# Seven block products for eight in three places of a four-layer graph network

## The chip, the cores and the metric

One core of a Trainium2 chip runs the whole program. The metric is device time in microseconds (us), the median of several executions of the same kernel; lower is better. All runs told here were in the fast state. "Rounds" are timed runs of a kernel in turn with the kernel before on the same chip. A ratio is the mean time of one kernel's fast runs over that of the other's in the same rounds, so it is not quite the ratio of the medians quoted beside it.

## The reference, cut to what matters

32 batches pass through four layers of a graph network in float32. A batch has 512 nodes with 128 features and a 512 x 512 adjacency matrix. In outline, with the parts that the change touches:

```python
# layer 2: four projections; the k-th sees the newest features and stored ones
src = nodes @ ws + bs            # 3rd: nodes = [f2, f1], 4th: [f3, f1, f0]
dst = nodes @ wd + bd
src_agg = einsum(src, l2norm(adj, 2)); dst_agg = einsum(dst, l2norm(adj, 1))
f_new = tanh(concat(src_agg, self_rep, dst_agg) @ wu + bu)

# layer 3: a GRU; r and z gates add two products
r = sigmoid(h @ W_hr + m @ W_ir + b_r)
z = sigmoid(h @ W_hz + m @ W_iz + b_z)
```

The rest is cut. h1 is the normed input of layer 1, f0 that of layer 2, f1 to f4 the outputs of layer 2's projections, h and m the state and the message of layer 3. The four weight matrices of such a place form a 2 x 2 block matrix, and the two halves of the 512 nodes make the left side 2 x 2 blocks as well: eight block products.

## The kernel before

The order of instructions is not written down by hand. A planner inside the kernel runs when the program is built: it goes through time with a price for every operation, gives each engine the most urgent ready one, and hands out buffers. The result is one fixed list per engine, and **each engine works through its list strictly in order**. The prices and the rule for buffers matter below:

```python
class Plan:
    RATE, TRANSFER = 240.0, 1.3     # a transfer lands after kb / 240 + 1.3 us
    ...
    # in order(): may this operation take its buffers now?
    older = item[1].batch - min(unfinished)
    if any(len(free[x.kind]) < len([y for y in new if y.kind == x.kind])
           + older * self.kept.get(x.kind, 0) for x in new):
        held.append(item)           # no: looked at again later
        continue

plan = Plan(sb, psum, {"bank": 8, "s2": 32, "s4": 6, "s8": 10},   # places
                      {"bank": 1, "s2": 7, "s4": 0, "s8": 0})     # kept, per older batch
def t_mm(n):  return n * 0.001675 + 0.004
def t_act(n, pointers=0):  return 0.09 + 0.093 * pointers + n / 1150
```

A batch that is not the oldest unfinished one may take a buffer only if `older * kept` of that kind stay free. The large kind, s8, holds the adjacency matrices and the gates.

Two pieces of a batch matter below. `turned` transposes a 512 x 128 matrix: VectorE turns 32 x 32 blocks, four transfers write them to HBM, one reads them back, and ScalarE copies the result into the order that matmuls need. The copy `rows` spreads the norms of the adjacency matrix:

```python
for k in range(NC):
    op("SP", 0.4, lambda k=k: away(k), [blk], [(bounce, {k})], kb=64)
op("SP", 0.4, lambda: nc.sync.dma_start(mT.ap(), bounce.tile), [bounce], [mT], kb=256)
...
op("ACT", t_act(N), lambda: nc.scalar.copy(hT..., turned_cols(t)), [t], [hT])
...
op("ACT", t_act(2 * N), lambda: nc.scalar.copy(
    rows.ap().rearrange("p s (c n) -> p (s c) n", c=NC),
    spaced.ap().rearrange("p n k -> p k n")), [spaced], [rows])
```

The first three and the last two batches transpose on TensorE instead (`at_ends`). A projection of layer 2 (`paired_rows`) makes, for each half of the nodes, products of 256 columns that add up in one PSUM bank, and one VectorE addition of the bias writes `sd`, which the aggregation then uses.

## Time and profile before

| | before |
|---|---|
| median of 4 runs (range) | 2353.82 us (2352.41 to 2356.74) |
| profiled span, granted clock | 2352.6 us, full in the middle |
| TensorE (PE) / VectorE (DVE) / ScalarE (ACT) busy | 2321.2 / 1123.3 / 923.2 us |
| distance of equal batches in the middle | 71.66 us |

The prediction below shows the lines for these. Three more lines also belong here. They are from the list of transfers (`--dma`); the last columns are size and the median us from issue to landing. f4r is the same round trip for f4.

```profile
turned<-turn_turned SPq DMA_DIRECT2D x81, 256.0 KB, 2.6
spaced<-bounce SPq DMA_DIRECT2D x32, 512.0 KB, 4.1
f4r<-turn_f4r SPq DMA_DIRECT2D x27, 256.0 KB, 4.6
```

The planner prices 256 KB at 256 / 240 + 1.3 = 2.37 and 512 KB at 512 / 240 + 1.3 = 3.43 us. So the trace showed before any change that the prices are too low, most of all for f4r.

### The profile page before, as it was taken

How to read it: one execution, taken by the hardware profiler on the slowest of the kernel's cores; microseconds unless marked ns; L12 is line 12 of the kernel's file. 1: busy time of each engine (PE TensorE's matmuls, PEld its weight loads, DVE VectorE, ACT ScalarE, POOL GpSimd, SP SyncE). 2: the span in 40 equal slices, each digit the busy share in tenths (PEclk: the TensorE clock that was granted, in tenths of full speed). 3: DMA queues.
4: the chain of work that ended last, by engine and by line, in shares of the span. 5: the costliest groups of instructions: out<-in, count | busy, mean ns of one | idle time of the engine just before them, and what ended most of it. 6: DMA issues, size and time to landing. Idle time of an engine off the chain costs nothing.

```text
span 2352.6 us, 24187 instructions
## 1 busy us (share of the span) xinstructions
PE 2321.2 (99%) x8466; PEld 1426.5 (61%) x8466; DVE 1123.3 (48%) x2917; ACT 923.2 (39%) x2018; POOL 282.0 (12%) x218
## 2 busy tenths in 40 slices
PE   6999999999999999999999999999999999999998
PEld 4665566566666565665666665656665666656655
DVE  4344444555445555445554445554455544454523
ACT  7424233443334443334443344433344333344312
POOL 3100011111011110011110111110111101111001
PEclk9999999999999999999999999999999999999999
DMA  6112212322313332223223133322233321332000
GB/s 239 59 54 72 72 52 92 108 86 88 99 56 104 90 99 90 75 78 108 90 90 99 50 103 91 98 90 82 72 107 90 98 91 55 98 107 72 17 10 9
DMA packets 127128, 196.36 MB, mean 83 GB/s; under 512 B 18336, under 2 KB 75040, under 8 KB 127008
## 3 DMA queue, kind: packets, MB, share of 16 engines
q1 hardware_dynamic: 126720, 194.71, 27.0%
q8 instruction: 66, 1.08, 0.2%
q14 instruction: 54, 0.44, 0.1%
q10 hardware_dynamic: 288, 0.13, 0.0%
HBM read 157.95 MB, written 36.83 MB: 83 GB/s over the span
## 4 chain that ended last, share of the span: by engine, by line
PE 94%; DVE 2%; ACT 2%; DMA 1%; issue 0%; POOL 0%; SPq 0%; DVEq 0%; POOLq 0%; ACTq 0%
PE ps_agg L289 62%; PE ps_sd L289 18%; PE ps_gate L289 7%; PE ps_upd L289 3%; PE ps_msg L289 1%; PE ps_lin L289 1%; PE ps_node L289 1%; ACT h L417 1%; POOL sc L405 0%; DMA a<-in_adj 0%; ACT sq L581 0%; DVE bn L389 0%; SPq L435 0%; DVE g L659 0%; DMA spaced<-bounce 0%
## 5 line engine op out<-in xcount | busy, mean ns | idle before, releaser
L289 PE MATMUL ps_agg<-aT,sd 128*128 128x512 f32 x1024 | 521.2, 593 | 0.0
L289 PE MATMUL ps_agg<-a,sd 128*128 128x512 f32 x1024 | 501.1, 592 | 0.0
L289 PE MATMUL ps_sd<-w_sb,f 128*128 128x256 f32 x1792 | 484.2, 381 | 1.0 <-ACT f L455 0.8
L490 DVE TENSOR_TENSOR sd<-ps_sd,rf_sb 128x512 f32<-128x512 f32 x256 | 175.9, 687 | 606.7 <-PE ps_sd L289 606.7
L289 PEld LDWEIGHTS ps_sd<-w_sb,f 128*128 128x128 f32 x1792 | 327.1, 191 | 172.8 <-issue 134.0
L405 POOL TENSOR_TENSOR sc<-v,neg_half 128x4 f32<-128x4 f32 (+1 forms) x128 | 180.1, 1408 | 2020.1 <-DVE v L392 1384.0
L417 ACT ACTIVATE h<-xr,nb,sc 128x128 f32<-128x128 f32 x384 | 157.9, 482 | 556.8 <-DVE nb L413 556.6
L289 PEld LDWEIGHTS ps_agg<-a,sd 128*128 128x128 f32 x1024 | 185.4, 191 | 164.3 <-issue 155.3
L289 PEld LDWEIGHTS ps_agg<-aT,sd 128*128 128x128 f32 x1024 | 187.1, 191 | 84.4 <-issue 56.9
L289 PE MATMUL ps_agg<-f,w_sb 128*128 128x512 f32 x448 | 229.7, 594 | 0.0
L619 ACT ACTIVATE f<-ps_agg,cf_sb 128x512 f32<-128x512 f32 x128 | 87.2, 681 | 132.0 <-PE ps_agg L289 131.9
L289 PE MATMUL ps_agg<-aT,rep 128*128 128x512 f32 x256 | 131.4, 595 | 3.6 <-DVE rep L557 3.6
L289 PEld LDWEIGHTS ps_gate<-w_sb,mT 128*128 128x128 f32 x512 | 95.3, 190 | 61.6 <-issue 55.0
L426 DVE STREAM_TRANSPOSE blk<-h 128x512 f32<-128x512 f32 x81 | 57.6, 711 | 154.8 <-ACT h L417 154.8
L289 PE MATMUL ps_agg<-a,rep 128*128 128x512 f32 x256 | 130.7, 592 | 0.0
L289 PE MATMUL ps_agg<-aT,msg 128*128 128x512 f32 x256 | 125.9, 592 | 0.0
L289 PE MATMUL ps_gate<-w_sb,mT 128*128 128x256 f32 (+1 forms) x512 | 123.1, 326 | 0.0
L289 PEld LDWEIGHTS ps_gate<-w_sb,hT 128*128 128x128 f32 x512 | 91.0, 190 | 49.8 <-issue 43.5
L289 PE MATMUL ps_gate<-w_sb,hT 128*128 128x128 f32 (+1 forms) x512 | 119.0, 327 | 0.0
L289 PE MATMUL ps_agg<-aT,h 128*128 128x256 f32 (+2 forms) x384 | 108.8, 380 | 0.0
L603 DVE TENSOR_TENSOR aT<-aT,rows 128x512 f32<-128x512 f32 x128 | 87.8, 687 | 35.4 <-PE ps_agg L289 33.8
L669 ACT ACTIVATE g<-g 128x512 f32<-128x512 f32 (+1 forms) x68 | 41.1, 605 | 156.1 <-DVE g L659 156.1
(101 smaller groups left out, 2724.6 us busy)
## 6 DMA issues: line engine op xcount, KB each, us to landing
aT<-in_adjt SPq DMA_DIRECT2D x124, 512.0 KB, 4.8
a<-in_adj SPq DMA_DIRECT2D x62, 512.0 KB, 4.6
turn_turned<-blk SPq DMA_DIRECT2D x324, 64.0 KB, 1.8
turned<-turn_turned SPq DMA_DIRECT2D x81, 256.0 KB, 2.6
spaced<-bounce SPq DMA_DIRECT2D x32, 512.0 KB, 4.1
x<-in_x SPq DMA_DIRECT2D x32, 256.0 KB, 2.9
out<-xo SPq DMA_DIRECT2D x30, 256.0 KB, 3.0
turn_f4r<-blk SPq DMA_DIRECT2D x108, 64.0 KB, 2.3
```

Source lines behind the costliest of these rows:

```text
L289: op("PE", t_mm(n), lambda: nc.tensor.matmul(out_of(ps.ap()), lhs(), rhs(), start=start, stop=stop), reads, [ps], later=later)
L405: op("POOL", t_pow(n), lambda: nc.gpsimd.tensor_tensor(inv.ap()[:, :n], v8.ap()[:, :n], neg_half[:, :n], op=ALU.pow), [v8, NH], [(inv, {0})])
L417: op("ACT", t_act(D, 2), lambda c=c: nc.scalar.activation(h.ap()[:, c, :], xin.ap()[:, c, :], AF.Relu, bias=nb.ap()[:, c:c + 1], scale=inv ...
L426: op("DVE", t_tt(N), lambda: nc.vector.transpose(blk.ap().rearrange("p b (c r) -> p c b r", c=NC), m.ap().rearrange("p c (b s) -> p c b s" ...
L490: op("DVE", t_tt(N), lambda ps=ps, h=h: nc.vector.tensor_add(sd.ap()[:, 2 * h:2 * h + 2, :], ps.ap().rearrange("p (j v) -> p j v", j=2), a ...
L603: op("DVE", t_tt(N), lambda m=m, c=c, s=s: nc.vector.tensor_mul(m.ap()[:, c, :], m.ap()[:, c, :], rows.ap()[:, s, :]), [(m, {c}), rows], [ ...
L619: op("ACT", t_act(N, 1), lambda ps=ps, i=i, f_new=f_new: nc.scalar.activation(f_new.ap(), ps.ap(), AF.Tanh, bias=cf_sb[:, i:i + 1]), [ps, ...
L669: op("ACT", t_act(cols), lambda s=s: nc.scalar.activation(g.ap()[:, s, :2 * D], g.ap()[:, s, :2 * D], AF.Tanh, scale=0.5), [(g, part)], [( ...
```

## The change

The intent: seven block products (a scheme of Strassen's kind) and some additions on VectorE for eight products on TensorE, which is the bound. Places: layer 2's third projection ("mid"), its fourth ("last"), and the r and z gates of layer 3 ("gates", except in the last two batches). The core of the diff:

```diff
+SEVEN = {"last": 0 * 5 * D, "mid": 1 * 5 * D, "gates": 2 * 5 * D}
-    plan = Plan(..., {"bank": 1, "s2": 7, "s4": 0, "s8": 0})
+    plan = Plan(..., {"bank": 1, "s2": 5, "s4": 0, "s8": 1})
     def t_mm(n):
-        return n * 0.001675 + 0.004
+        return n * 0.00166 + 0.0085
+        def seven(site, x1, x2, dst, part):
+            ... # five buffers s13, s24, ev, dv, xx; four PSUM banks
+            dve(of(s13, 1), lambda: half(x1, 0), lambda: half(x1, 1), [x1], ..., sub=True)
+            product(bank_a, 0, lambda: half(x1, 0), lambda: wt(b11), [x1, wbuf])
+            product(bank_a, 1, of(s13, 1), lambda: t(2), ...)
+            ... # five more products, each two matmuls of 128 columns,
+            ... # and thirteen more VectorE additions
         for i, (wsd, wn) in enumerate(W_L2):
-            sd = paired_rows(f, wsd, W2F, rf_sb, RF, i * 2 * D)
+            if i == 2 and "mid" in SEVEN:
+                sd = buf("s4", (P, NC, 2 * D), "sd")
+                seven("mid", f[1], f[0], *of_halves(sd))
+            elif i == 3 and "last" in SEVEN:
+                sd = paired_rows(f[:1], wsd, W2F, rf_sb, RF, i * 2 * D, early)
+            else:
+                sd = paired_rows(f, wsd, W2F, rf_sb, RF, i * 2 * D)
 ... # (cut) gates alike; combined weights at setup; finer parts of buffers
```

Besides the products, the change alters what the planner keeps back: of the large buffers now one for each older unfinished batch. With 0, the planner finds no end for three places (that version doesn't build). Of the small ones (s2) it keeps 5 instead of 7, and a matmul's price changes a little.

## The prediction

> **What bounds the kernel now.** I read the page first: the engines' shares, then the chain that ended last.
>
> ```profile
> PE 2321.2 (99%) x8466; PEld 1426.5 (61%) x8466; DVE 1123.3 (48%) x2917; ACT 923.2 (39%) x2018; POOL 282.0 (12%) x218
> ...
> PE 94%; DVE 2%; ACT 2%; DMA 1%; issue 0%; POOL 0%; SPq 0%; DVEq 0%; POOLq 0%; ACTq 0%
> ```
>
> TensorE is busy for 2321.2 of 2352.6 us, and 94% of the chain is matmuls. Busy alone doesn't prove a full pipe, since matmuls overlap; so I went on to the chain in order of time and to the busy times of two stretches.
>
> ```profile
> 341.00 8.59 PE ps_agg L289 x20
> 352.16 2.16 PE ps_sd L289 x10
> 370.70 1.34 PE ps_upd L289 x12
> 412.66 8.59 PE ps_agg L289 x20
> ```
>
> ```profile
> 341.00:412.66 71.66, 71.66 (x261) 43.98 (x261) 35.40 (x91) 28.61 (x62) 8.80 (x7) 1.00 0.28 89
> 412.66:484.32 71.66, 71.66 (x261) 43.99 (x261) 35.39 (x91) 28.61 (x62) 8.80 (x7) 1.00 0.30 89
> ```
>
> The same long piece returns every 71.66 us: one batch of the 32. In the second fence the columns are length, then busy (records) of PE, weight loads, VectorE, ScalarE, GpSimd, then clock, DMA share, GB/s. TensorE is busy in all of it and its clock is full. The chain also gives the price of a matmul inside a stream. Each float32 matmul leaves two records. 512 columns: 8.59 / 10 = 0.859 us. 256 columns: 2.16 / 5 = 0.432. 128 columns: 1.34 / 6 = 0.223. For 384 columns the timeline has 0.64.
>
> Does this price list explain a batch? Dividing the record counts of the groups, kept apart by shape, by 64 gives per batch 52 matmuls of 512 columns, 42 of 256, 2 of 384 and 34 of 128: together 130, as the x261 above says. 52 x 0.859 + 42 x 0.432 + 2 x 0.64 + 34 x 0.223 = 71.67 us, against 71.66. So a batch in the middle is the sum of its matmuls and nothing else: what is taken off that sum comes off the time one for one, until something else takes its place. What is not full is the two ends:
>
> ```profile
> PE ps_fold L289 <- DMA raw<-in_raw: 11.1, 1, 11.1
> PE ps_t L453 <- ACT h L417: 3.6, 2, 2.3
> PE ps_agg L289 <- DVE rep L557: 3.6, 3, 1.5
> ```
>
> These are TensorE's largest waits (total, times, longest). All its idle time is 2352.6 - 2321.2 = 31.4 us, of which 11.1 is the first load.
>
> **What the Trainium skill says.** "FP8 and Floating Point Precision", section TensorE Precision Notes: true FP32 takes 4 passes through the array. "TensorE: Matmul & The Clock Gate", section Back-to-back issue gap: an isolated warm gap of N/2.4 + 2.5 ns per instruction. Two records of two passes at 512 columns would be 2 x (2 x 512/2.4 + 2.5) = 858 ns: the trace agrees (859). At 128 columns it would be 218 ns, and the trace has 223; the same section warns that at small N the weight loads are part of the spacing. I take the trace's 223. "VectorE: DVE Perf Modes", section The TRN2 errata: a float32 tensor_tensor add lasts (N + 151)/0.96 ns; 691 ns at 512, which the trace shows (690 for the bias addition after the msg product). For 256 it gives an estimate of 424 ns; the trace has no such shape yet, and between its 340 (128) and 684 (512) a straight line gives 455.
>
> **The change part by part.** In three places a product of a (2x2 blocks) left side with a 2x2 block weight, eight block products, becomes seven plus additions on VectorE.
>
> Removed: per place 8 matmuls of 256 columns, 8 x 0.432 = 3.456 us. Added: 14 of 128 columns (7 products, each for two blocks of 128 rows), 14 x 0.223 = 3.122 us. Saved: 0.334 us a place, less than the eighth of 3.456 (0.432), because 14 short instructions pay the fixed part more often than 8 long ones. The third and fourth projection of layer 2 do it in all 32 batches, the gates in 30 (the last two keep the old form): 94 places. The static order confirms the counts: 752 matmuls of 256 columns go, 1316 of 128 come. 94 x 0.334 = 31.4 us, all on the path by the argument above. In the middle a batch should take 71.66 - 3 x 0.334 = 70.66 us.
>
> VectorE: per place 12 additions of 256 columns and 2 of 512, 12 x 0.424 + 2 x 0.691 = 6.47 us. Gone are 2 of 512 per third projection and 2 per gate site, 124 in all; the fourth projection keeps its two, now adding to the stored half instead of the bias. Sum: 94 x 6.47 - 124 x 0.687 = +523 us, so about 1646 us busy, 71% of the new span; in a middle batch 35.4 + 19.4 - 2.8 = 52 of 70.7 us. That is beside TensorE, not on the path, as long as the answers come in time. ScalarE, GpSimd and the transfers hardly change (one small bias load more). Setup gains 15 additions of 128 columns on VectorE, 15 x 0.34 = 5 us, at a time when it is busy half (24 of the first 50 us).
>
> Does VectorE answer in time? The place that feeds at once is the third projection: its newest input arrives, a subtraction must be ready before the second pair of products, and the sums before the aggregation. Between the first use of that input and the product that needs the subtraction, the order holds 512 + two 128 + 512 columns, 0.859 + 0.446 + 0.859 = 2.16 us, for one addition of 0.42 and a handover. The fourth projection's products start a layer earlier, from inputs known since layer one, so they are filler. A middle batch is the same pattern of matmul rows again and again, and in it a second half of an already begun fourth-projection product (needing only f0 and weights) is left over for 74 rows and run late: the scheduler, which picks the most urgent ready instruction, had ready work throughout. So the order has no planned hole there.
>
> At the ends nothing hides the longer detour through VectorE. The first batches and the last two run with little beside them; I put 1 us for each end, an estimate from the waits above (single waits of 0.5 to 2.3 us there) and from a few more dependent additions of about 0.4 us.
>
> Sum: 2353.8 - 31.4 + 2 = 2324.4; I go to 2323, since some added delay at the ends may fall where TensorE waits anyway.
>
> **The rivals.**
> Weight loads bound the short products. A load lasts 190 ns in the trace and a 128-column record takes only 111 ns of the stream. Were they exposed, a short matmul would cost 2 x 190 = 380 ns and the change would add 1316 x 0.157 = 207 us. Against it: the strings of twelve 128-column matmuls with new stationary blocks each time run at 0.223 us now. I give it almost nothing.
> VectorE becomes the bound, or its answers come late. Its load goes from 49% to some 74% of a batch, in an order fixed beforehand. If each place stalled TensorE by a single late addition (0.33 us), the whole gain would be gone: about 2354. For it: a chain of dependent additions with waits on itself in the order. Against it: the slack above, and that the same scheduler produced a middle without holes before. I expect at most a third of that, 10 us.
> The full arithmetic gain. Without the fixed cost a place saves 0.427 us (256 columns less), 40 us in all: 2314. The trace's 128-column price speaks against it.
> More than 2%: it would need 47 us, more than the arithmetic allows, so 15 us of the 31.4 idle would have to go as well, though 11.1 of them wait for the first load, which is not touched.
>
> **Range and chances.** 2323 us, 1.3% below 2353.8. Downward, better filling at the ends or a price nearer the full gain could bring 7 us: 2316. Upward, stalls in a third of the places and at the ends: 2337. Within 2% means 2306.8 to 2400.9. Faster by over 2%: 0.03; slower: 0.02; within: 0.95.
>
> **What would show it.** Right: equal distance of the chain's long pieces, 70.6 to 70.7 us instead of 71.66, with TensorE busy throughout; the new 128-column products 0.22 us apart; VectorE near 1650 us; TensorE's idle total 31 to 35 us. Wrong: waits of TensorE for VectorE (the s24, s13 or sd pieces) repeating in every batch; a gap between new products above 0.23 us; a beginning or an end that is 5 us or more longer.

## The result, and the profile after

Measured: **2360.76 us** (median of 4, 2356.81 to 2364.68) against 2353.82. The ratio is 1.0028, 95% interval 1.0008 to 1.0048: slower by 0.3%, the same within the 2% limit. The prediction had said 2323 with a range of 2316 to 2337. The time is outside it.

The page of the changed kernel, engines' shares and the chain that ended last:

```profile
PE 2306.8 (98%) x9594; PEld 1440.2 (61%) x9594; DVE 1543.5 (65%) x4124; ACT 937.8 (40%) x2018; POOL 255.6 (11%) x218
...
PE 77%; DMA 9%; DVE 5%; ACT 4%; SPq 2%; issue 1%; POOL 1%; ACTq 0%; POOLq 0%; DVEq 0%
```

TensorE has 14 us less to do by this count, and matmuls fell from 94% to 77% of the chain; transfers, VectorE and ScalarE took the rest. The chain in order of time, and the busy times of one batch and of a long stretch (columns as in the prediction):

```profile
1236.56 6.87 PE ps_agg L295 x16
...
1308.37 6.87 PE ps_agg L295 x16
...
1379.91 6.87 PE ps_agg L295 x16
```

```profile
1236.56:1308.37 71.81, 71.20 (x297) 44.33 (x297) 48.88 (x132) 29.89 (x65) 7.58 (x6) 1.00 0.29 88
600.00:1200.00 600.00, 593.71 (x2473) 369.90 (x2472) 404.28 (x1072) 243.62 (x522) 64.48 (x51) 1.00 0.30 89
```

The equal pieces are 71.81 and 71.54 us apart, not 70.66, and TensorE is no longer full. TensorE's waits, by what it waited for (total, times, longest):

```profile
PE ps_sd L295 <- ACT hT L488: 14.9, 25, 2.0
PE ps_fold L295 <- DMA raw<-in_raw: 10.7, 1, 10.7
PE ps_t L483 <- ACT h L447: 6.0, 5, 2.3
PE ps_sd L295 <- ACT f L488: 4.1, 6, 1.5
PE ps_agg L295 <- POOL diag L618: 2.9, 2, 1.6
PE ps_agg L295 <- DVE sd L522: 2.8, 5, 0.8
```

The top line is new: once in each of 25 middle batches the first product of layer 1 waits for ScalarE's copy of the transposed h1. The timeline around one of them in the changed kernel (start, duration, engine; in brackets the idle time before and what ended it):

```profile
1009.25 3.24 SPq L465 DMA_DIRECT2D turn_turned<-blk  x7
...
1012.67 0.34 SPq L469 DMA_DIRECT2D turned<-turn_turned  x1
...
1014.93 1.02 PE L295 MATMUL ps_agg<-aT,sd 128*128 128x512 f32 x2
...
1015.52 0.62 ACT L488 COPY hT<-turned 128x512 f32<-128x512 f32 x1 [4.94 <-DMA turned<-turn_turned]
...
1016.20 1.99 PE L295 MATMUL ps_sd<-w_sb,hT 128*128 128x256 f32 x8 [0.25 <-ACT hT L488]
```

and the same place in the kernel before:

```profile
1064.92 0.34 SPq L439 DMA_DIRECT2D turned<-turn_turned  x1
...
1067.52 0.62 ACT L458 COPY hT<-turned 128x512 f32<-128x512 f32 x1 [0.29 <-DMA turned<-turn_turned]
...
1067.76 1.02 PE L289 MATMUL ps_agg<-f,w_sb 128*128 128x512 f32 x2
...
1068.62 1.67 PE L289 MATMUL ps_sd<-w_sb,hT 128*128 128x256 f32 x7
```

Before, the copy ended at 1068.14, and TensorE came to the product at 1068.62, just when the two 512-column records before it were through (1067.76 + 2 x 0.429). After, those two would have been through at 1014.93 + 0.86 = 1015.79, but the copy ended only at 1016.14, so the product began at 1016.20: 0.41 us late, of which the page's idle time shows 0.25, because the shown ends of records reach into the next.

So busy time hides part of a stall here. "Perfetto Trace Analysis", section Identifying the Most-Contended Engine, warns that matmul busy time is not a good measure of how close a kernel is to the roofline, because pipelined matmuls look smaller in the trace. That it is no good measure, this trace confirms; but here a record looks longer than its share: one of 512 columns is shown 0.59 us long, and the next starts 0.43 us after it. I therefore counted stalls from start to start: each matmul's start, less the start before, less the usual distance for that shape (0.429 us for a record of 512 columns, 0.216 for 256, 0.111 for 128). What is left below 40 ns a record adds up to under 2 us in any trace, so the price list holds in all of them. It splits the spans so:

| us, from the traces | before | after |
|---|---|---|
| sum of the matmuls at the price list | 2308.5 | 2276.6 |
| stalls, first 150 us (without the first wait) | 15.9 | 20.2 |
| stalls, 150 to 2150 us | 5.8 | 40.2 |
| stalls, after 2150 us | 3.4 | 7.4 |
| TensorE from a batch's first to its last matmul (mean of 18) | 250 | 206 |

The work fell by 31.9 us, and the stalls rose by 42.7. The difference, 10.8, is the growth of the span (2362.9 - 2352.6 = 10.3) but for the two ends. A part of these stalls is clock. After many of the longer stalls the granted clock is at half for 3.4 or 6.8 us, and matmuls that run at half clock count as late here. A stretch of only_mid (one of the runs below; the clock is the third number from the end):

```profile
526.80:533.60 6.80, 6.08 (x16) 4.32 (x17) 2.51 (x8) 1.65 (x4) 1.01 (x1) 0.50 0.00 0
```

By a count from the clock records, this is some 7 of the changed kernel's 67.8 us of stalls and 3 of the 25.1 before, most of it in the first 150 us; but it is some 40 of the 134 us in the middle of only_mid and 15 of the 77 of copy_priced. All 18 half-clock stretches in the middle of only_mid start within 2 us of the end of a stall of 2.7 us or more. Before, last_priced and reserve_fifth, without such stalls in the middle, have no half-clock stretch there.

The last row of the table is the other thing that the traces show: a batch lives 44 us shorter on TensorE. With a batch every 72 us that is 2.9 batches side by side instead of 3.5.

### The profile page after: what moved, and what is told of

It is laid out like the page before. It is cut to its first block, busy times and chain, and to the rows that moved or that the text cites. A ratio compares the mean times of both kernels' runs of the same rounds, so it can differ in the third digit from the quotient of the medians.

```text
span 2362.9 us, 28102 instructions
## 1 busy us (share of the span) xinstructions
PE 2306.8 (98%) x9594; PEld 1440.2 (61%) x9594; DVE 1543.5 (65%) x4124; ACT 937.8 (40%) x2018; POOL 255.6 (11%) x218
## 4 chain that ended last, share of the span: by engine, by line
PE 77%; DMA 9%; DVE 5%; ACT 4%; SPq 2%; issue 1%; POOL 1%; ACTq 0%; POOLq 0%; DVEq 0%
PE ps_agg L295 52%; PE ps_sd L295 9%; PE ps_seven L566 8%; DMA turned<-turn_turned 4%; PE ps_upd L295 4%; PE ps_gate L295 2%; SPq L465 2%; ACT h L447 1%; DMA spaced<-bounce 1%; DMA turn_turned<-blk 1%; PE ps_node L295 1%; PE ps_msg L295 1%; DMA bounce<-inv 1%; DVE blk L456 1%; DMA f4r<-turn_f4r 1%
## 5 line engine op out<-in xcount | busy, mean ns | idle before, releaser
L435 POOL TENSOR_TENSOR sc<-v,neg_half 128x4 f32<-128x4 f32 (+1 forms) x128 | 151.8, 1186 | 1595.7 <-DVE v L422 1224.1
L295 PE MATMUL ps_sd<-w_sb,f 128*128 128x256 f32 x768 | 219.0, 383 | 5.6 <-ACT f L488 4.1
L566 PEld LDWEIGHTS ps_seven<-t_sb,s 128*128 128x128 f32 x1128 | 157.9, 191 | 67.0 <-issue 57.4
L295 PEld LDWEIGHTS ps_sd<-w_sb,f 128*128 128x128 f32 x768 | 132.3, 192 | 75.7 <-issue 55.5
L522 DVE TENSOR_TENSOR sd<-ps_sd,rf_sb 128x512 f32<-128x512 f32 x128 | 88.1, 688 | 123.0 <-PE ps_sd L295 122.8
L566 PE MATMUL ps_seven<-t_sb,s 128*128 128x128 f32 x1128 | 164.5, 275 | 0.0
L704 ACT COPY rows<-spaced 128x1024 f32<-128x1024 f32 x32 | 65.9, 2059 | 205.6 <-DMA spaced<-bounce 205.6
L566 PEld LDWEIGHTS ps_seven<-w_sb,f 128*128 128x128 f32 x512 | 82.4, 191 | 73.1 <-issue 65.1
L607 ACT ACTIVATE sq<-a 128x512 f32<-128x512 f32 x128 | 80.1, 626 | 113.8 <-DMA a<-in_adj 112.0
L708 DVE TENSOR_TENSOR a<-a,rows 128x512 f32<-128x512 f32 x128 | 87.8, 689 | 13.2 <-PE ps_agg L295 11.7
```

Of the source, the lines that this page charges most:

```text
L295: op("PE", t_mm(n), lambda: nc.tensor.matmul(out_of(ps.ap()), lhs(), rhs(), start=start, stop=stop), reads, [ps], later=later)
L435: op("POOL", t_pow(n), lambda: nc.gpsimd.tensor_tensor(inv.ap()[:, :n], v8.ap()[:, :n], neg_half[:, :n], op=ALU.pow), [v8, NH], [(inv, {0})])
L522: op("DVE", t_tt(N), lambda ps=ps, h=h: nc.vector.tensor_add(sd.ap()[:, 2 * h:2 * h + 2, :], ps.ap().rearrange("p (j v) -> p j v", j=2), s ...
L566: op("PE", t_mm(D), lambda j=j: nc.tensor.matmul(ps.ap()[:, k * H + j * D:k * H + (j + 1) * D], lhs()[:, j * P:(j + 1) * P], rhs(), start= ...
L607: op("ACT", 0.73, lambda c=c: nc.scalar.activation(sq.ap(), a.ap()[:, c, :], AF.Copy, accum_out=stat.ap()[:, c:c + 1]), [(a, {c})], [sq, ( ...
L704: op("ACT", t_act(2 * N), lambda: nc.scalar.copy(rows.ap().rearrange("p s (c n) -> p (s c) n", c=NC), spaced.ap().rearrange("p n k -> p k ...
```

## The experiments

All 18 gave correct results. "Middle" is the stalls between 150 and 2150 us, "life" the last row of the table above.

| run | seven-product places | kept s8 | prices (copy, landing) | median us | ratio | middle | life |
|---|---|---|---|---|---|---|---|
| before | none | 0 | old | 2353.8 | 1 | 5.8 | 250 |
| after | three | 1 | old | 2360.8 | 1.0028 | 40.2 | 206 |
| plan18 | three | 1 | old, 1.8 | 2356.9 | 1.0007 | 32.1 | 204 |
| copy_twice | three | 1 | old | 2373.4 | 1.0079 | 56.8 | 208 |
| copy_twice_before | none | 0 | old | 2364.4 | 1.0036 | 15.0 | 251 |
| h1_on_tensor | three | 1 | old | 2346.0 | 0.9960 | 13.0 | 204 |
| no_place | none | 0 | old | 2350.5 | 0.9983 | 3.3 | 250 |
| only_last | last | 0 | old | 2359.9 | 1.0024 | 23.7 | 251 |
| only_mid | mid | 0 | old | 2462.7 | 1.0469 | 134.1 | 268 |
| only_gates | gates | 0 | old | 2355.7 | 1.0004 | 20.2 | 251 |
| last_priced | last | 0 | 2.0, 1.65 | 2337.5 | 0.9925 | 0.8 | 256 |
| mid_priced | mid | 0 | 2.0, 1.5 | 2338.7 | 0.9930 | 1.9 | 251 |
| three_priced | three | 1 | 2.0, 1.8 | 2359.0 | 1.0017 | 32.6 | 204 |
| last_gates_priced | two | 1 | 2.0, 1.65 | 2355.6 | 1.0007 | 22.3 | 204 |
| small_reserve | three | 0.12 | old | 2371.1 | 1.0068 | 54.7 | 255 |
| small_reserve_priced | three | 0.25 | 2.0, 1.65 | 2328.5 | 0.9887 | 11.2 | 250 |
| last_reserved | last | 1 | 2.0, 1.65 | 2363.6 | 1.0038 | 18.2 | 205 |
| copy_priced | three | 0.34 | 2.0, old | 2409.4 | 1.0243 | 77.2 | 255 |
| landing_priced | three | 0.25 | old, 1.65 | 2365.7 | 1.0044 | 46.9 | 255 |
| reserve_fifth | three | 0.2 | 2.0, 1.8 | 2317.6 | 0.9843 | 1.8 | 251 |

The old prices are 0.98 us for the copy `rows` and 1.3 us for the landing part of a transfer.

### First round: the way of h1

The first theory was that the new order has no slack at the transposed h1 and its round trip through HBM is priced too low. The rival was VectorE's additional work.

**plan18** raises the landing price, so that the planner expects transfers later.

```diff
-    RATE, TRANSFER = 240.0, 1.3
+    RATE, TRANSFER = 240.0, 1.8
```

> The changed kernel with one number of its own scheduler altered: the fixed time that it assumes for a transfer to land, 1.3 us, becomes 1.8. The instructions are the same, only their order moves. Theory (the transposed h1, fetched back by DMA, lands 0.4 to 0.9 us later than the scheduler assumed, and the order left nothing between): TensorE's stalls in the middle, 39 us in the changed kernel, fall under 15 us, and the time falls by 25 to 35 us, to 2325 to 2335. Rival (VectorE, 65% busy, answers late): transfers have nothing to do with it, the stalls stay and so does the time, 2350 to 2365.

Measured: 2356.9 us, a miss. The waits on h1 shrank to some 3 us, but others came up elsewhere in the new order: 12.7 us at products that wait for VectorE's `sd`, 6.5 for ScalarE's tanh of layer 2. The price of the landing alone is not the cause.

**copy_twice** and **copy_twice_before** let ScalarE copy the transposed h1 twice, without the planner knowing, in the changed kernel and in the kernel before.

```diff
-            op("ACT", t_act(N), lambda: nc.scalar.copy(hT..., turned_cols(t)), [t], [hT])
+            def copy():
+                for _ in range(reps):        # 2 for h1
+                    nc.scalar.copy(hT..., turned_cols(t))
+            op("ACT", t_act(N), copy, [t], [hT])
```

> The changed kernel, order untouched, with the ScalarE copy of the transposed h1 issued twice, which the scheduler does not know of: 0.54 us more between the landing of the transfer and TensorE, in 27 batches. Theory: there is no slack at that place, so each batch loses about 0.5 us more: 27 x 0.54 = 15 us, 2370 to 2378. Rival (VectorE late): ScalarE is 40% busy, and its extra copy costs at most 3 us.

> The same doubled copy in the kernel before, where the first product from h1 starts 0.3 to 0.55 us after the copy ends in nearly all middle batches (0.05 is the least seen). Theory: 0.54 us eats that slack of 0.3 to 0.5 and leaves 0.05 to 0.3 us a batch: 2 to 8 us longer, 2356 to 2362, clearly less than the same dose costs in the changed kernel. Rival: 0 to 3 us, the same as in the changed kernel.

Measured: +12.6 us on the changed kernel (2373.4), as expected. On the kernel before +9 by the medians of these rounds (2364.4), a miss: 2 us above what was expected, and not clearly less than in the changed kernel. Its waits were 0.1 to 0.5 us in 25 batches, where the changed kernel's rose from a median of 0.7 to 1.3 us. So both orders are close to their limit at this product; the one before had just enough slack (0.48 us in the batch shown), the one after none.

**h1_on_tensor** takes the round trip away: h1 is transposed by TensorE in every batch, as at the ends.

```diff
-        def transposed(h, name):
-            if at_ends:
+        def transposed(h, name, pe=False):
+            if at_ends or pe:
...
-        h1T = transposed(h1, "hT")
+        h1T = transposed(h1, "hT", True)
```

> The changed kernel with h1 alone turned on TensorE in all batches, as the first three and last two already do: no transfer stands before the first product of layer 1. It adds 27 x 4 transposes of about 0.11 us, 12 us of TensorE. Theory: the 21 us of stalls at that product go, so 2345 to 2355 (a new order may bring its own stalls). Rival (VectorE late): the stalls stay and the 12 us are added: 2368 to 2375.

Measured: 2346.0 us, a hit and the first version faster than both kernels, if by only 0.4%. It pays 12 us of transposes on TensorE and still gains, because the middle's stalls fall from 40.2 to 13.0.

### Second round: each place alone

```diff
-SEVEN = {"last": 0 * 5 * D, "mid": 1 * 5 * D, "gates": 2 * 5 * D}
+SEVEN = {"last": 0 * 5 * D}       # or mid, or gates, or none
-    {"bank": 1, "s2": 5, "s4": 0, "s8": 1}
+    {"bank": 1, "s2": 5, "s4": 0, "s8": 0}
```

> The changed program with none of the three places in the new form; it differs from the kernel before only in the constants of the planner (matmul price, buffers kept back). Theory (the new form saves the PE time it should, and what eats it is an order that leaves no slack for the turned h1): the planner's own end of PE work falls from 2342.8 (kernel before) to 2338.8 us, and the kernel before ended 11 us after its plan, so 2345 to 2352 us, with under 5 us of waits on the turned h1. Rival (the new constants of the planner themselves do the harm, whatever the products): 2360 or more, with 20 us of waits on the turned h1.

> Only layer 2's fourth projection in the new form, 32 places: 32 x 0.334 = 10.7 us of PE work less than no_place. Theory (slack): in this plan the product on the turned h1 is not the next thing PE has to do, so no wait on it; plan end 2325.0 plus the 11 us of the kernel before: 2332 to 2341 us. Rival (each place stalls PE by itself, through VectorE's late sums, and the 43 us of extra stalls are shared by the three places, some 14 us each): 2350 to 2358 us.

> Only layer 2's third projection in the new form, the place whose sums feed at once, 32 places. Theory (slack): plan end 2330.5 plus 11 us: 2337 to 2347 us, waits on the turned h1 under 5 us. Rival (each place stalls PE by itself, this one most): 2350 to 2365 us, with the stalls at products that wait for VectorE's subtractions and sums.

> Only layer 3's r and z gates in the new form, 30 places. Theory (slack): plan end 2327.9 plus 11 us: 2335 to 2345 us. Rival (each place stalls by itself): 2350 to 2358 us.

Measured: no_place 2350.5 us, as expected. The three others missed: 2359.9, 2462.7 and 2355.7. None of them waits on h1 in the middle, where its copy is ready 7 us or more ahead; that part was right. But each has a repeating stall somewhere else. The rival seemed to win until I followed one back. In only_mid, TensorE loses 3.05 us at one product in most batches, and the timeline of only_mid tells why:

```profile
1137.94 0.45 SPq L699 DMA_DIRECT2D spaced<-bounce  x1
...
1142.23 2.04 ACT L704 COPY rows<-spaced 128x1024 f32<-128x1024 f32 x1 [3.89 <-DMA spaced<-bounce]
...
1144.17 0.61 ACT L488 COPY hT<-turned 128x512 f32<-128x512 f32 x1
...
1144.69 0.63 ACT L677 ACTIVATE y<-u 128x512 f32<-128x512 f32 x1
...
1145.35 0.69 DVE L679 TENSOR_TENSOR xr<-xr,y 128x512 f32<-128x512 f32 x1 [3.20 <-ACT y L677]
...
1148.59 2.08 PE L295 MATMUL ps_agg<-a,sd 128*128 128x512 f32 x2 [2.88 <-DVE sd L544]
```

The delay does not start at one of the new additions. A transfer of 512 KB lands 4.26 us after its issue (planned 3.43); ScalarE's list has the copy `rows` next, so it sits idle for it; the copy then takes 2.04 us where the planner has 0.98; behind it in ScalarE's list stands `y`; VectorE's list has the addition with `y` next, and sits idle 3.2 us, with the last sums of the third projection, which TensorE needs, some operations behind it. One late arrival has passed through three fixed lists. The copy lasts so long in every batch of every version; in the changed kernel:

```profile
L704 ACT COPY rows<-spaced x32: 2031/2059/2080, 38.1 to 2224.1; 128x1024 f32<-128x1024 f32 x32
```

(minimum, median and maximum in ns). In only_last the same copy delays a tanh of the gates, and VectorE behind it stalls TensorE 0.7 us a batch.

### Third round: two prices nearer to the traces

```diff
-        op("ACT", t_act(2 * N), lambda: nc.scalar.copy(      # rows
+        op("ACT", 2.0, lambda: nc.scalar.copy(
-    RATE, TRANSFER = 240.0, 1.3
+    RATE, TRANSFER = 240.0, 1.65          # mid_priced 1.5, three_priced 1.8
```

No instruction changes by this, only the order. last_gates_priced keeps 6 instead of 5 of the s2 buffers and drops "mid" from SEVEN.

> only_last again, with two prices of the planner set nearer to what the traces show: the ScalarE copy rows<-spaced 2.0 us instead of 0.98 (it lasts 2.05), and the landing part of a transfer 1.65 us instead of 1.3. No instruction changes, only the order. Theory (the saving is real, and mispriced steps in a fixed order eat it): the waits of only_last on VectorE's sd (16.5 + 2.7 us) shrink to under 6 us in all; plan end 2325 to 2330 us plus the 11 us that the kernel before ends after its plan: 2334 to 2343 us. Rival (the new form itself stalls TensorE, whatever the order): 2355 to 2362 us as only_last.

> only_mid again, with the same ScalarE copy priced 2.0 us and the landing 1.5 us. Theory (in only_mid a batch loses 3 us because this copy and the turned h1 arrive late in ScalarE's fixed order, behind which VectorE's last sums wait): the loss of 108 us goes nearly whole, 2338 to 2352 us. Rival (the third projection, which feeds at once, stalls TensorE by VectorE's own chain of additions): 2430 us or more.

> The changed kernel with the copy priced 2.0 us and the landing 1.8 us; it differs from plan18 only in the copy's price. Theory: VectorE's and ScalarE's late answers of plan18 (12.7 + 6.5 us) shrink; plan end 2318.5 us plus some 11 to 18 us: 2328 to 2340 us. Rival (with all three places the additions themselves make VectorE late): 2350 to 2360 us as plan18.

> Last and gates in the new form, third projection as before, the copy priced 2.0 us and the landing 1.65 us. 62 places x 0.334 = 20.7 us less PE work than no_place. Theory: plan end 2322 us plus some 11 to 18 us: 2333 to 2342 us, the best so far. Rival (each place stalls by itself): 2350 to 2362 us.

Measured: last_priced 2337.5 and mid_priced 2338.7, both hits; three_priced 2359.0 and last_gates_priced 2355.6, both misses. For a single place, the stretch from 600 to 1200 us is full (last_priced; TensorE was busy for 595.30 us of it in only_last):

```profile
600.00:1200.00 600.00, 600.00 (x2289) 371.81 (x2288) 338.02 (x874) 245.75 (x511) 66.94 (x51) 1.00 0.29 88
```

and against no_place the gains are 13.0 and 11.8 us, where the predicted price of a place gives 32 x 0.334 = 10.7 (no_place has the old prices, so a part of the 13.0 and 11.8 may be theirs). So the saving of a place is real, also of the one that feeds at once. But with two or three places the same prices did not help. These two runs also kept one large buffer back per older batch, and their batches live 204 us, not 250. That had to be told apart from the number of places.

### Fourth round: the reserve

```diff
-    {"bank": 1, "s2": 5, "s4": 0, "s8": 1}
+    {"bank": 1, "s2": 5, "s4": 0, "s8": 0.12}     # or 0.2, 0.25, 0.34
```

Because the planner compares free buffers with `needed + older * kept`, a kept share of 0.12 to 0.25 means one large buffer in all while one to four older batches are unfinished (0.34: two from three older ones on), and 1 means one for each of them. last_reserved is last_priced with 1 for 0.

> The changed kernel with one number changed: the planner keeps 0.12 instead of 1 of the ten large buffers (s8) back for each older batch that is unfinished; its prices stay. In the plans a batch then occupies TensorE from its first to its last product for 246 us instead of 201 (250 in the kernel before). Theory (the reserve took away the work that TensorE could turn to): no waits on the turned h1, whose planned slack is 5.7 us instead of 0.2. The mispriced copy may still stall elsewhere, as in only_last: 2325 to 2352 us, below the 2360.8 of the changed kernel in any case. Rival (three places in the new form make VectorE's answers late by themselves): 2355 us or more.

> All three places, 0.25 of a large buffer kept back for each older batch, and the ScalarE copy priced 2.0 us and the landing 1.65 us: both suspected causes mended at once. TensorE's work is that of the changed kernel; plan end 2304.7 us with no idle time in the middle. Theory: 2304.7 plus the 8 to 11 us that last_priced and the kernel before ended after their plans: 2312 to 2322 us, no stalls in the middle, VectorE 1540 us busy beside it. Rival (VectorE): 2345 us or more.

> last_priced with one number changed the other way: a whole large buffer kept back for each older batch, as in the changed kernel. Theory (the reserve does the harm): TensorE's span of a batch falls from 256 to 203 us in the plan, waits on the turned h1 or on VectorE come back in most batches, and with the 10 us of holes already in its plan (end 2339.1): 2352 to 2372 us. Rival (one place in the new form can't be hurt by it; the harm of the changed kernel comes from having three): 2335 to 2346 us.

Measured: small_reserve 2371.1, a miss. small_reserve_priced 2328.5, a miss by 6 us above its range, but 26 below the kernel before. last_reserved 2363.6, a hit: with nothing but the reserve raised, one place goes from 2337.5 to 2363.6 us, and the waits on h1 and on layer 2's tanh are back in some twelve batches each. Of these 26 us, some 12 are holes in its plan (end 2339.1 against 2327.3); the rest are stalls against it.

small_reserve missed for the reason of only_mid: no wait on h1 at all, as expected, but 33.6 us of stalls in 24 batches for the last sums of the third projection. The chain that ended last, in order of time, for one of them:

```profile
1165.87 4.27 DMA spaced<-bounce
...
1170.16 0.67 ACT rows L704
...
1170.92 1.20 issue
1172.12 0.62 ACT hT L488
...
1173.11 0.68 DVE dv L579
```

The transfer, the copy (only its first part is counted here; the rest appears as "issue"), then ScalarE's next entry, then VectorE. It remained open which of the two prices the small reserve needs, and whether small_reserve_priced was a lucky order.

> All three places, a reserve of 0.34 and only the ScalarE copy rows<-spaced priced 2.0 us; the landing stays at 1.3. In the plan a batch spans 243 us of TensorE, plan end 2307.4 us. In small_reserve the chain of the stalls runs from the landing of spaced over this copy to hT, to VectorE and to TensorE. Theory (the copy is the price that matters most once the reserve is small): the stalls at sd fall from 37 + 9 us to under 15: 2322 to 2338 us. Rival (the landing of transfers matters more): 2350 us or more.

> small_reserve_priced with the ScalarE copy at its old price of 0.98 us; the landing stays at 1.65. Plan end 2304.4 us. Theory (copy): its 1.07 us too little per batch come back as a wait, 27 batches x 1 us or more: 2345 to 2372 us. Rival (landing): close to small_reserve_priced, 2325 to 2335 us.

> small_reserve_priced with the landing priced 1.8 instead of 1.65 us and a reserve of 0.2 instead of 0.25: another order of the same kind (plan end 2304.8 us, planned slack of the turned h1 15.6 instead of 14.6 us). If what is left in small_reserve_priced (4.6 + 0.9 us of waits on sd in 9 batches) is a mispriced landing, it goes: 2318 to 2326 us. If it is chance of the order, 2322 to 2335 us. If lowering the reserve helped only by luck of one order, 2345 us or more.

Measured: landing_priced 2365.7, a hit; without the copy's price its 1.07 us come back as 37.8 us of stalls in 25 batches. copy_priced 2409.4, a clear miss: I had taken the copy for the price that matters. Its chain shows the other one:

```profile
1169.31 5.64 DMA f4r<-turn_f4r
...
1185.80 4.34 DMA spaced<-bounce
1190.17 2.05 ACT rows L704
```

A read-back planned at 2.37 us landed after 5.64; the median of f4r in this run is 4.2. So with the reserve small both prices seem to be needed, but this is the weaker half: copy_priced also keeps back 0.34 and not 0.25, a part of its loss is clock, and it is another order as well. That one price alone makes it worse by so much need not hold for another.

reserve_fifth, expected at 2318 to 2326 us at best, took **2317.6 us** (2316.2 to 2320.8), 1.6% less than the kernel before (ratio 0.9843, 95% interval 0.9828 to 0.9859: clear of noise, though the same within the 2% limit). Its page, its stretch and its chain in order of time:

```profile
PE 2288.0 (99%) x9594; PEld 1437.4 (62%) x9594; DVE 1517.4 (66%) x4124; ACT 937.3 (40%) x2018; POOL 266.5 (12%) x218
...
PE 96%; DVE 2%; ACT 1%; issue 0%; POOL 0%; DMA 0%; SPq 0%; DVEq 0%; ACTq 0%; POOLq 0%
```

```profile
600.00:1200.00 600.00, 600.00 (x2503) 376.13 (x2502) 406.43 (x1093) 250.95 (x541) 65.76 (x50) 1.00 0.31 93
```

```profile
351.15 8.58 PE ps_agg L295 x20
...
421.81 8.58 PE ps_agg L295 x20
...
492.48 8.58 PE ps_agg L295 x20
```

The same 9594 records as in the changed kernel, TensorE full, VectorE nearly as busy beside it as in the changed kernel, and the long pieces 70.66 and 70.67 us apart. Only three numbers of the planner differ from the changed kernel.

## Why the prediction was wrong, and where it was right

- **"A batch in the middle is the sum of its matmuls and nothing else"**: right for the kernel before. Its second half, "until something else takes its place", is what happened.
- **The saving**: 31.4 us predicted, 31.9 found (2308.5 - 2276.6). The short products are 0.22 us apart, so the weight loads stay hidden, and the rivals of exposed loads and of the full arithmetic gain fall, as predicted.
- **VectorE's load**: predicted 1646 us, the page has 1543.5. The 256-column additions have a mean of 0.41 to 0.42 us, as estimated. But the prediction added single durations to the page's busy time, which joins overlapping records. By single durations the load rose from 1286 to 1781 us: 494 more, where 523 were predicted. A batch has 47.5 busy (reserve_fifth), where 52 were predicted.
- **"Does VectorE answer in time?"** is the step that failed, with its conclusion "the scheduler, which picks the most urgent ready instruction, had ready work throughout. So the order has no planned hole there." There was no planned hole, true (the planner of the changed kernel, run again, leaves TensorE 0.8 us idle between 150 and 2150 us). But I took that for slack. In an order fixed ahead, what counts is how late an answer may come before its engine has nothing else to do, and against which price it was planned. I looked only at VectorE, whose answers only follow; late were transfers and a ScalarE copy, which the text had set aside as "hardly change". Middle stalls: 40.2 us, where I gave at most "a third" of 31; by the list of waits 14.9 us are at the product that waits for ScalarE's copy of h1, 25 times, and only 2.8 are waits for VectorE's `sd`.
- **"The same scheduler produced a middle without holes before"**: it was the same planner with another reserve. The line of the diff that keeps one large buffer per older batch is not in the prediction at all. last_reserved against last_priced shows what it does: the batch's life falls from 256 to 205 us and the time rises by 26.
- **The rival "its answers come late"** named the right form of the loss ("the whole gain would be gone: about 2354") with the wrong sender. reserve_fifth settles it: with all of VectorE's additional work there, the middle has 1.8 us of stalls.
- **The ends**: 2 us predicted, 8.3 found (4.3 + 4.0). In reserve_fifth the ends have as little as before (15.7 and 3.2), so they too belong to the order.
- **The predicted time itself** was reachable: 2353.8 - 31.9 and 4.3 us fewer stalls than before (20.8 instead of 25.1) give 2317.6, which is what reserve_fifth takes.

What the runs show, then, is two causes that work together. With the large reserve the planner keeps fewer batches side by side, and its order has the product on h1 next when h1 is just due (planned slack 0.2 us, on record with small_reserve, which has 5.7). And two prices are too low (transfers, and the copy by 1.07 us), so that in the tight orders tried here something came late and the fixed lists handed it on. How the reserve comes to take the slack is argued, not shown: a long life alone doesn't give it. The kernel before has a life of 250 us, and h1's copy ends only 0.4 us ahead of its product (median); no_place has the same life, and 17 us. With the reserve at 1, no price brought the saving (three_priced, plan18); with the old prices, a smaller reserve didn't help (small_reserve); with reserve and prices mended, the whole saving is there in one order (2317.6) and most of it in another (2328.5). "Perfetto Trace Analysis", section Optimization Strategy, says that the same gap repeating on the engine that should be full can mean that there isn't enough memory for the next tile; the wait on h1 in 25 batches was such a gap, and the number of buffers held back was part of its cause (last_reserved brings it back in some twelve batches, small_reserve takes it away).

Not settled: how the 42.7 us divide between the two causes, since each setting gives another order; and whether the kernel before also gains by better prices alone (no run tried it).

## What to carry to other kernels

When an order is planned ahead, a change of the work is also a change of the order: compare every price of the planner with the durations in the trace, and read the diff's buffer numbers as carefully as its instructions. An order without holes in the plan is not one with slack; ask of each product on the full engine how late its input may be, and how long what brings it really takes. If a saving doesn't appear, count the work and the stalls apart (start to start), then follow one repeating stall back through the lists to the first thing that was late.

## What the Trainium skill lacked or had wrong

- "DMA: Bandwidth & Descriptors", section Anatomy of one DMA — SWDGE (gpsimd) path: its fit of 2.0 us plus bytes at 436 GB/s gives an estimate of 2.6 us for 256 KB and 3.2 for 512 KB. It is given for transfers issued by GpSimd; those here are issued by SyncE, so this is no test of it. The read-back of `turned` comes to the same (medians 2.6 and 2.7 us), that of f4r, of the same size, lies above (4.6 before, 3.6 after), and so do the 512 KB transfers (3.6 to 5.4 in the changed kernel). The fit has no term for other transfers in flight; whether they are the reason, no run here shows.
- "VectorE: DVE Perf Modes", section The TRN2 errata: its row for ScalarE gives (224 + n) / 1.2 ns for a copy. For 512 columns that is 613 ns, and the copy of h1 lasts 0.61 to 0.62 us. For the 1024 columns of `rows`, 1040 ns, but it lasts 2.05 us. That copy reads with a stride of 32 bytes; "SBUF — State Buffer", section Specifications (TRN2), says of its 16-byte cachelines that each cross to a new line pays a penalty, without a size. That the stride is the reason is argued, not shown by a run.
- "VectorE: DVE Perf Modes", section The TRN2 errata: its formula for a float32 addition gives 424 ns at 256 columns; the 1129 additions of that shape in the changed kernel have a mean of 417. It holds within 2%.
- "TensorE: Matmul & The Clock Gate", section Back-to-back issue gap: the isolated formula gives 218 ns for a float32 matmul of 128 columns, the runs 223 with a weight load for each record. Its sustained 81 ns for a matmul of 128 columns with its load would make 162 for the two passes of a record; a record with one load takes 111. Its sustained 131 ns at 512 columns would make 524 for four passes; the trace has 859, which the isolated formula gives, though the page says that it over-counts there.
- No page says what a fixed order does with a late arrival: 1 us on ScalarE, in its place in the list, cost TensorE 1.5 us a batch (landing_priced, 37.8 us in 25 batches).
